# A gated cross-attention and FFN layer on one core: x loaded transposed with a centred Wq, first loads and projections in parts, sums beside weighted sums, and a list-scheduled FFN tail

## The chip, the cores and the metric

The kernel runs on one core of a Trainium2 chip. The metric is the device time of one execution in microseconds. Three executions of the kernel before took 3187.14, 3182.26 and 3186.66 us, median 3186.66. The core has five instruction queues that this kernel uses: TensorE (PE; its weight loads are listed as PEld), VectorE (DVE), ScalarE (ACT), GpSimd (POOL) and SyncE (SP), which issues every DMA. Each works through its instructions in order and waits on semaphores for the others.

## The reference, cut to what matters

x is 32 sequences of 224 tokens with 512 features, the context 32 sequences of 750 keys with 384 features; 16 heads of 32.

```python
q = layernorm(x) @ Wq.T                       # 16 heads of 32
k, v = ctx @ Wkv.T
attn = softmax(where(mask_of_query, q k^T / sqrt(32), -1e9))
x = x + tanh(g_xattn) * (attn @ v)
h = bitlinear(layernorm(x), w1, b1)           # 512 -> 2048
x = x + tanh(g_ffn) * bitlinear(gelu(h), w2, b2)
# bitlinear: rmsnorm, then each token is rounded to 8 bits with the scale
# 127/max|.|, weights to -1, 0, 1 with the mean of |w|, matmul, bias
```

A token's layernorm needs the mean and variance of its 512 features, a token's rounding needs the maximum of its row, and softmax needs the maximum and the sum over 750 keys.

## The kernel before, in words

The work is a sequence of N = 128 steps (b, g): sequence b and a group g of four heads. Three rows of PSUM tiles matter: `ps_s`, one tile of four banks for scores, and `ps_m`, four tiles of one bank for everything else.

A step has two halves that are worked on in neighbouring steps. `maxima` makes the scores with queries on the partitions, a third at a time (tile sm), and DVE reduces each third to maxima (mx). `minus_max` turns these into three bf16 parts (nb), `turn_max` transposes them (pn, nT). `weights` then makes the scores again with keys on the partitions (tile se: first minus the maximum, by a product with ones, then k by q), ACT takes the exponential (p), and POOL adds the p up over the keys (acc, five additions a step). `values` multiplies v by p (the left half of the tile po), `sums` multiplies ones by acc (the right half of the same po), ACT copies both to oT, and `finish` transposes oT (pyt), divides, and POOL adds the result to x in SBUF; after the last group of a sequence x goes to a DRAM tensor x1_d.

Queries come from `q_units`: DVE takes mean and variance (`stats`), POOL the factor 1/sqrt(variance) times mask and 1/sqrt(32) (`scale`, ve), DVE makes xn = (x - mean) * ve (`apply`), `turn` transposes xn on TensorE in two groups of four (pxn) and ACT copies it (xnT), `q_piece` multiplies by Wq (pq) and ACT copies the result (qT). `k_units` makes k of a step in two halves (pk), `v_piece` makes v in pieces (pv_None, or pv for a half piece).

The FFN takes tiles of 128 tokens in NF = 28 pairs, from `ffn_units`. A pair's first part loads x1_d (`load`, xg), takes statistics, centres (xc), finds the row maximum (amax), rounds (`grid` on POOL, which also adds b2 to xg; `round` on ACT) and transposes by DMA (`turn`, xq to xT). Each of its two tiles t then has four products with w1 (units b, tile ph; DVE scales and adds b1 into h), gelu, square with the sum of squares, row maxima (hm), scales (sb0, sb1, sb2, mostly small POOL operations with a Newton iteration in `rsqrt`), rounding (`cgrid` on POOL, `cround` on ACT, tile hq), a DMA transpose (`cturn`, hT) and two products with w2 (units c, tile po from w2q and hT; DVE adds into xg), after which xg is stored.

The order of all instructions is written out by the loop over steps. Each step has six slots k. In an even slot `maxima` of the next step comes first, in an odd one `weights` of this step; then the units that a `put` marks first, then FFN units as far as they fit, then the other units. So between one sm and the next se (and between se and the next sm), which share the one `ps_s` tile, TensorE has the slot's units to do while DVE reduces or ACT exponentiates. `PE_ROOM` (2.7 us in even, 2.2 in odd slots, less what the slot's units are said to take) limits what FFN work `Ffn.fill` puts in; each FFN unit names the unit that it follows and a lag in slots. In steps 0 to 11 the three odd slots hold the quantisation of w1 and w2 (`weight_units`) in place of FFN units. Slots before: 0 turn_max and the first k half; 1 `values`; 2 the second k half; 3 `sums`; 4 `finish`; 5 a piece of v of the next sequence; slots 3 and 4 also hold half pieces of v (g = 0, 1) or `q_piece` (g = 2, 3), and slots 0 and 2 of g = 1 the two `turn`. Ahead of the loop stand the loads, all q pieces of sequence 0, k of two steps and four pieces of v. Behind it, `fill` is called until the FFN is empty, the newest pair first.

SP takes its DMAs in the order in which these units are written out; a DMA whose data is not there yet holds all behind it.

Of the kernel before, what the change touches and what calls it, by code (L numbers as in the profile page):

```python
# [24 lines left out]
def flamingo_gated_layer(  # L25
    ctx: ExitStack,
    tc: tile.TileContext,
    x: bass.AP,
    ctxT: bass.AP,
# [45 lines left out]
    x1_d = dram.tile([NT, D], F32, name="x1_d")  # L75

# [30 lines left out]

    def rsqrt(pool, v, n, p, tag):


        y = pool.tile([P, n], F32, tag=f"{tag}_y", name=f"{tag}_y")[:p]
        a = pool.tile([P, n], F32, tag=f"{tag}_a", name=f"{tag}_a")[:p]
        gp.tensor_scalar(
            y.bitcast(I32), v.bitcast(I32), -0.5, float(0x5F3759DF), ALU.mult, ALU.add
        )
        for _ in range(3):
            gp.tensor_tensor(a, y, y, ALU.mult)
            gp.tensor_tensor(a, a, v, ALU.mult)
            gp.tensor_scalar(a, a, -0.5, 1.5, ALU.mult, ALU.add)
            gp.tensor_tensor(y, y, a, ALU.mult)  # L120
        return y
# [18 lines left out]
    np_ = pool("xn", 1)  # L140
# [3 lines left out]
    smp = pool("small", 2)  # L144
    HB, XG = 2, 2
# [3 lines left out]
    fp = pool("f", 1)  # L149
    ps_s = pool("ps_s", 1, PSUM)  # L150
# [13 lines left out]
    x_of, y_of, q_of, k_of, v_of = {}, {}, {}, {}, {}  # L164
# [4 lines left out]
    def load_y(b):  # L169
        y_of[b] = yp.tile([P, NYC, M], F32, tag="y", name=f"y_{b}")  # L170
        sp.dma_start(y_of[b], ctxT[b].rearrange("(c p) m -> p c m", p=P))
# [4 lines left out]


    def q_units(b):

# [3 lines left out]
        xn = np_.tile([CP, NQ, D], F32, tag="xn", name=f"xn_{b}")  # L183
        xnT = np_.tile([P, NDC, S], F32, tag="xnT", name=f"xnT_{b}")
# [13 lines left out]
        def apply():  # L198
            for t in range(NQ):
                dve.tensor_scalar(  # L200
                    xn[:, t, :], x_of[b][:, t, :], mv[:, t, 0:1], ve[:, t : t + 1],
                    ALU.subtract, ALU.mult,
                )

        def turn(c2):
            pt = ps_m.tile([P, 2, NQ, CP], F32, tag="m", name=f"pxn_{b}_{c2}")
            for i in range(2):
                c = 2 * c2 + i
                for t in range(NQ):
                    pe.transpose(  # L210
                        pt[:, i, t, :], xn[:, t, c * P : (c + 1) * P], ident[:CP, :CP]
                    )
            act.copy(xnT[:, 2 * c2 : 2 * c2 + 2, :], pt.rearrange("p c t n -> p c (t n)"))

        def q_piece(g):
            pq = ps_m.tile([P, 512], F32, tag="m", name=f"pq_{b}_{g}")
            for c in range(NDC):
                pe.matmul(
                    pq[:, :S], wq_sb[:, c, g * P : (g + 1) * P], xnT[:, c, :],
                    start=(c == 0), stop=(c == NDC - 1),  # L220
                )
            act.copy(qT[:, g, :], pq[:, :S])

        return [stats, scale, apply], [lambda i=i: turn(i) for i in range(2)], [
            lambda g=g: q_piece(g) for g in range(NG)
        ]
# [153 lines left out]
    def sums(b, g):  # L380
# [7 lines left out]
        oT = smp.tile([P, 2 * S], F32, tag="oT", name=f"oT_{b}_{g}")  # L388
# [3 lines left out]
    def finish(b, g):  # L392
# [11 lines left out]
        yo = smp.tile([CP, NQ, P], F32, tag="yo", name=f"yo_{b}_{g}")  # L404
# [8 lines left out]
        if g == NG - 1:  # L413
            sp.dma_start(
                x1_d[b * S : (b + 1) * S, :].rearrange("(t p) d -> p t d", p=CP), x_of[b]
            )
# [73 lines left out]
    def quant_scales(s, r, amax, n, tag, unit):  # L490
# [7 lines left out]
        gp.tensor_tensor(a, r, amax, ALU.mult)  # L498
        gp.tensor_scalar(a, a, 1e-5, None, ALU.max)
# [3 lines left out]
        gp.tensor_scalar(c, c, 127.0, None, ALU.mult)  # L503
        gp.tensor_tensor(c, c, r, ALU.mult)
        gp.tensor_scalar(a, a, unit, None, ALU.mult)

    def ffn_units(i):
# [6 lines left out]
        def a_load():  # L514
            s["xg"] = xgp.tile([P, TG, D], F32, tag="xg", name=f"xg_{i}")
            sp.dma_start(s["xg"], x1_d[rows, :].rearrange("(t p) d -> p t d", p=P))
# [8 lines left out]
        def a_rsqrt():  # L525
# [4 lines left out]
            gp.tensor_scalar(s["nm"], s["mv"][:, :, 0], -1.0, None, ALU.mult)  # L530
            gp.tensor_scalar(ve, s["mv"][:, :, 1], 1.0 + EPS, EPS * EPS, ALU.mult, ALU.add)
# [18 lines left out]
        def a_grid():  # L550
            for t in range(TG):
# [3 lines left out]
                )  # L555

# [33 lines left out]
        def b_square(t):  # L590
            h = s["h", t]
            junk = fp.tile([P, F], BF16, tag="xc", name=f"junk_{i}_{t}")
# [9 lines left out]
        def c_scales(t, k):  # L602
            if k == 0:
# [3 lines left out]
                gp.tensor_scalar(u, s["ssq", t], 1.0 / F, EPS, ALU.mult, ALU.add)  # L607
# [12 lines left out]
        def c_turn(t):  # L620
            s["hT", t] = fp.tile([P, NFC, P], BF16, tag="hT", name=f"hT_{i}_{t}")
            sp.dma_start_transpose(s["hT", t], s.pop(("hq", t)))

        def c_matmul(t, half):
# [8 lines left out]
            if half:  # L633
                at = (i * TG + t) * P
                sp.dma_start(out[at : at + P, :], s["xg"][:, t, :])
# [10 lines left out]
            ("grid", 0, "sa2", 0, 0, 0, a_grid),  # L646
            ("round", 2, "grid", 0, 1.1, 0, a_round),
# [3 lines left out]
        for t in range(TG):  # L651
            part = []
            for f in range(4):
                part.append((
                    f"b{t}{f}", 0 if f else 3, f"b{t}0" if f else "turn", 0.9, 0, 0.75,
# [12 lines left out]
            for a in range(2):  # L668
# [3 lines left out]
                ))  # L672
            parts.append(part)
        return parts

    class Ffn:
# [9 lines left out]
        def ready(self, pair, unit):  # L686
            name, lag, after = unit[:3]
            if after is not None:
                at = self.at.get((pair, after))
                if at is None or self.slot < at + lag:  # L690
                    return False

            before = {
                "load": [(pair - XG, f"c{TG - 1}1")],
# [4 lines left out]
            if name[-1].isdigit():  # L699
# [7 lines left out]
                    f"cturn{t}": [(p1, f"c{t1}1")],  # L707
                }
            if name.startswith("square") and any(
# [41 lines left out]
        def done(self):  # L751
            return self.next == NF and not self.parts
# [146 lines left out]
```

## Time and profile before

The profiled execution took 3185.84 us, its span from first to last instruction is 3184.1 us, and the mean granted TensorE clock 0.984.

| Stretch, us | TensorE busy | DVE busy | ACT busy | POOL busy | granted clock |
|---|---|---|---|---|---|
| 0 to 44.7, ahead of the step loop | 31.8 | 13.1 | 6.8 | 4.1 | 1.00 |
| 66 to 150 | 81.0 | 51.1 | 31.5 | 47.3 | 1.00 |
| 150 to 350 | 182.9 | 134.8 | 71.8 | 118.8 | 0.97 |

Groups that the change touches: 256 transposes pxn, 259 ns each; 64 scalings xn, 1153 ns; 64 copies xnT, 532 ns; 128 copies qT, 345 ns; 1024 matmuls po from acc and ones. DMAs, median time to landing: x 448 KB 6.9 us, y 1125 KB 6.3, x_d 448 KB 3.1, xg 512 KB 3.6, out 256 KB 2.0, xT 2.5, hT 4.3.

Busy shares count an engine's instructions, and ends of matmuls are modelled. A wait is put down to the engine whose signal came last. "xN" is a number of instructions, and letters such as pk, sm, se, po are the tiles written. The line L51 is that of a helper (`Ordered`), which records every operation, so lines don't tell operations apart and tile names do.

### The profile page before, as it was taken

The page shows a single profiled execution, that of the slowest core. Times are in us where ns is not written, and L with a number is a line of the kernel's source. Part 1 is how long each engine was busy: PE and PEld are TensorE (multiplying, and loading weights), DVE is VectorE, ACT ScalarE, POOL GpSimd, SP SyncE. Part 2 cuts the span into 40 slices and gives each one's busy share as a digit, 9 for nine tenths or more (in the row PEclk, how much of TensorE's full clock was granted, in tenths as well). Part 3 has the DMA queues.
Part 4 walks back from the last instruction along what each step waited for, and adds up shares of the span by engine and source line. Part 5 has one row for each costly group of instructions (what it writes and reads, how often), then busy time and mean ns, then how long its engine had stood idle before and what let it go on. Part 6 is the DMA issues. An engine that isn't in the chain of part 4 may idle for free.

```text
span 3184.1 us, 63629 instructions
## 1 busy us (share of the span) xinstructions
PE 2996.3 (94%) x27522; PEld 1920.3 (60%) x27522; DVE 1705.7 (54%) x2501; ACT 1515.2 (48%) x1663; POOL 2069.3 (65%) x3048
## 2 busy tenths in 40 slices
PE   7998999999999999999999999999999999999963
PEld 5655556666666666666666666666666666666632
DVE  4676555555555555555555455465555554555442
ACT  2333444554545445544554454455444545554542
POOL 2564667766676676666766666776667667666672
PEclk9999999999999999999999999999999999999976
DMA  3322122011211111122011211111121011111111
GB/s 130 100 79 75 37 50 64 17 51 47 57 51 32 39 45 50 42 55 56 21 48 42 56 41 50 37 41 48 47 57 51 23 47 45 50 46 31 37 36 43
DMA packets 199753, 157.09 MB, mean 49 GB/s; under 512 B 150832, under 2 KB 150832, under 8 KB 199344
## 3 DMA queue, kind: packets, MB, share of 16 engines
q1 hardware_dynamic: 199472, 153.03, 17.4%
q8 instruction: 215, 3.52, 0.5%
q14 instruction: 66, 0.54, 0.1%
HBM read 86.94 MB, written 29.36 MB: 37 GB/s over the span
## 4 chain that ended last, share of the span: by engine, by line
PE 77%; DVE 14%; ACT 4%; POOL 3%; issue 1%; DMA 1%; SPq 0%; ACTq 0%; POOLq 0%; DVEq 0%
PE po L51 16%; PE se L51 13%; PE sm L51 12%; DVE mx L51 11%; PE pk L51 10%; PE pv_None L51 9%; PE ph L51 6%; PE pq L51 4%; PE pv L51 4%; ACT p L51 2%; ACT L51 1%; POOL acc L51 1%; PE pyt L51 1%; DVE xn L51 1%; PE pxn L51 1%
## 5 line engine op out<-in xcount | busy, mean ns | idle before, releaser
L51 POOL TENSOR_TENSOR acc<-acc,p 125x896 f32<-125x896 f32 x512 | 1070.1, 2090 | 462.8 <-ACT p L51 442.3
L51 DVE TENSOR_REDUCE mx<-sm 112x4 f32<-112x2000 f32 (+1 forms) x384 | 860.9, 2242 | 924.5 <-PE sm L51 924.5
L51 ACT ACTIVATE p<-se 125x1792 f32<-125x1792 f32 x384 | 638.9, 1664 | 426.4 <-PE se L51 416.3
L51 PE MATMUL pk<-y,wkv_sb 128*128 128x375 f32 x1536 | 537.7, 486 | 15.2 <-DMA wkv_sb<-in_wkvT 12.2
L51 ACT COPY kT<-pk 128x375 f32<-128x375 f32 x256 | 120.8, 472 | 716.8 <-PE pk L51 716.8
L51 PE MATMUL sm<-kT,qT 32*112 32x500 f32 (+1 forms) x4096 | 426.7, 508 | 30.2 <-ACT p L51 29.6
L51 POOL TENSOR_TENSOR acc<-p 125x896 f32<-125x896 f32 x128 | 267.1, 2087 | 257.4 <-ACT p L51 257.0
L51 PEld LDWEIGHTS pk<-y,wkv_sb 128*128 128x128 f32 x1536 | 278.7, 190 | 177.5 <-issue 32.9
L51 PE MATMUL pv_None<-wkv_sb,y 128*125 128x256 f32 x1536 | 366.1, 389 | 0.0
L51 PE MATMUL se<-qT,kT 32*125 32x224 f32 x6144 | 364.8, 349 | 0.0
L51 PEld LDWEIGHTS pv_None<-wkv_sb,y 128*125 128x125 f32 x1536 | 279.3, 188 | 70.9 <-issue 34.2
L51 PE MATMUL po<-p,v 125*32 125x224 f32 x6144 | 321.3, 358 | 0.1
L51 PEld LDWEIGHTS se<-qT,kT 32*125 32x125 f32 x6144 | 299.4, 183 | 0.2
L51 PE MATMUL po<-w2q,hT 128*128 128x256 fp8e4 x1792 | 224.6, 281 | 60.1 <-DMA hT<-hq 60.1
L51 DVE SCALAR_TENSOR_TENSOR h<-ph,qa_am,b_sb 128x512 f32<-128x512 f32 x224 | 164.8, 743 | 203.3 <-PE ph L51 202.2
L51 PEld LDWEIGHTS sm<-kT,qT 32*112 32x112 f32 x4096 | 159.2, 170 | 166.1 <-issue 99.9
L51 PEld LDWEIGHTS po<-p,v 125*32 125x32 f32 x6144 | 187.8, 111 | 115.6 <-issue 40.1
L51 PEld LDWEIGHTS <-hT 128*128 128x128 bf16 x1792 | 174.2, 101 | 104.2 <-DMA hT<-hq 62.3
L51 PE MATMUL ph<-w1q,xT 128*128 128x512 fp8e4 x896 | 226.8, 382 | 4.8 <-DVE h L51 4.8
L51 PE MATMUL pq<-xnT,wq_sb 128*128 128x224 f32 x1024 | 219.3, 357 | 0.2 <-ACT xnT L51 0.2
L51 PE MATMUL se<-nT,ones 3*125 3x448 bf16 x1536 | 157.4, 396 | 64.6 <-DVE mx L51 60.7
L51 POOL TENSOR_TENSOR x<-x,yo 112x256 f32<-112x256 f32 x128 | 100.9, 788 | 159.0 <-DVE yo L51 112.0
(96 smaller groups left out, 3207.6 us busy)
## 6 DMA issues: line engine op xcount, KB each, us to landing
y<-in_ctxT SPq DMA_DIRECT2D x32, 1125.0 KB, 6.3
x<-in_x SPq DMA_DIRECT2D x32, 448.0 KB, 6.9
x_d<-x SPq DMA_DIRECT2D x32, 448.0 KB, 3.1
xg<-x_d SPq DMA_DIRECT2D x28, 512.0 KB, 3.6
out<-xg SPq DMA_DIRECT2D x56, 256.0 KB, 2.0
wa<-in_w1T SPq DMA_DIRECT2D x8, 512.0 KB, 4.5
wa<-in_w2T SPq DMA_DIRECT2D x8, 512.0 KB, 4.0
wb<-in_w1T SPq DMA_DIRECT2D x8, 512.0 KB, 3.8
```

The lines of the kernel that those rows point to most:

```text
L51: return lambda *args, **kw: tc.keep_in_program_order(build(*args, **kw))
```

## The change

A second copy of x, transposed to features by tokens, is handed to the kernel (xT), and loaded per sequence into one SBUF tile. The mean is taken out of Wq instead of x: `centre` multiplies ones by Wq for its column sums and subtracts 1/512 of them. So `q_piece` multiplies the centred Wq by x^T, and each token's factor is applied to the product by DVE. The factor lies with tokens on partitions and is needed along the free dimension in all partitions; `spread` writes it to DRAM and reads it back to all partitions (for sequence 0 by a product with the identity). `apply` and `turn` are gone.

The first loads come in parts, the first 128 columns of Wkv and Wq and half of y first. Two q pieces of sequence 0 and all v pieces go into the steps' slots (`put_values`; one slot more in steps 0, 2, 3 and 4). The second k half moves from slot 2 to 1, `values` and `sums` stand together in slot 2, the store of x in slot 5. Small operations are fused where they have one column. The FFN's `bias` and `out` become units of their own, squares have their own tile, hT has two. The last pair is loaded from x in SBUF. After the loop `drain` writes all that is left of both pairs in an order chosen by estimated times (`TAKES_US`): among the units that can start within 1 us of the soonest, the one with the longest path behind it. The small operations then run on DVE instead of POOL.

```diff
+        m = pool.tile([P, n], F32, tag=f"{tag}_m", name=f"{tag}_m")[:p]
+        gp = small[0]
         gp.tensor_scalar(
             y.bitcast(I32), v.bitcast(I32), -0.5, float(0x5F3759DF), ALU.mult, ALU.add
         )
+        gp.tensor_scalar(m, v, -0.5, None, ALU.mult)
         for _ in range(3):
+            if n == 1:
+                gp.tensor_scalar(a, y, y, m, ALU.mult, ALU.mult)
+                gp.tensor_scalar(y, a, 1.5, y, ALU.add, ALU.mult)
+                continue
             gp.tensor_tensor(a, y, y, ALU.mult)
-            gp.tensor_tensor(a, a, v, ALU.mult)
-            gp.tensor_scalar(a, a, -0.5, 1.5, ALU.mult, ALU.add)
+            gp.tensor_tensor(a, a, m, ALU.mult)
+            gp.tensor_scalar(a, a, 1.5, None, ALU.add)
             gp.tensor_tensor(y, y, a, ALU.mult)
         return y
...
+    def load_xT(b):
+        xT_of[b] = xtp.tile([P, NDC, S], F32, tag="xT", name=f"xTb_{b}")
+        sp.dma_start(xT_of[b], xT[b].rearrange("(c p) s -> p c s", p=P))
+
+    def centre(lo, hi):
+
+
+        pw = ps_m.tile([P, 512], F32, tag="m", name=f"pwq_{lo}")
+        for c in range(NDC):
+            pe.matmul(
+                pw[:, : hi - lo], ones, wq_sb[:, c, lo:hi], start=(c == 0), stop=(c == NDC - 1)
+            )
+        for c in range(NDC):
+            dve.scalar_tensor_tensor(
+                wq_sb[:, c, lo:hi], pw[:, : hi - lo], -1.0 / D, wq_sb[:, c, lo:hi],
+                ALU.mult, ALU.add,
...
+        def spread():
+            if b == 0:
+                pr = ps_m.tile([P, NQ, CP], F32, tag="m", name="prb")
                 for t in range(NQ):
-                    pe.transpose(
-                        pt[:, i, t, :], xn[:, t, c * P : (c + 1) * P], ident[:CP, :CP]
+                    pe.matmul(
+                        pr[:, t, :], ve[:, t : t + 1].to_broadcast([CP, P]), ident[:CP, :CP],
+                        start=True, stop=True,
                     )
-            act.copy(xnT[:, 2 * c2 : 2 * c2 + 2, :], pt.rearrange("p c t n -> p c (t n)"))
+                act.copy(rb, pr.rearrange("p t n -> p (t n)"))
+                return
+            with nc.allow_non_contiguous_dma(reason="one number of each token"):
+                sp.dma_start(r_d[b].rearrange("(t p) -> p t", p=CP), ve)
+            sp.dma_start(rb, r_d[b].partition_broadcast(P))
...
-                    pq[:, :S], wq_sb[:, c, g * P : (g + 1) * P], xnT[:, c, :],
+                    pq[:, :S], wq_sb[:, c, g * P : (g + 1) * P], xT_of[b][:, c, :],
...
+            dve.tensor_tensor(qT[:, g, :], pq[:, :S], rb, ALU.mult)
...
+            if i < NF - 1:
+                sp.dma_start(s["xg"], x1_d[rows, :].rearrange("(t p) d -> p t d", p=P))
+                return
+            at = rows.start
+            while at < rows.stop:
+                (q, p), (t, to) = divmod(at, CP), divmod(at - rows.start, P)
+                n = min(CP - p, P - to)
+                sp.dma_start(
+                    s["xg"][to : to + n, t, :], x_of[q // NQ][p : p + n, q % NQ, :]
+                )
+                at += n
...
+    def store(b):
+        sp.dma_start(
+            x1_d[b * S : (b + 1) * S, :].rearrange("(t p) d -> p t d", p=CP), x_of[b]
+        )
...
+        def drain(self):
+
+
+            small[0] = dve
+            free = dict.fromkeys(("PE", "ACT", "DVE", "POOL", "SP"), 0.0)
+            end = {}
+
+            def takes(name):
+                kind = name.rstrip("0123456789")
+                return TAKES_US.get(kind + name[-1]) or TAKES_US[kind]
+
+            while self.next < NF:
+                self.parts += [[self.next, part] for part in ffn_units(self.next)]
+                self.next += 1
+            left = {}
+
+            def rank(at):
+
+                if at not in left:
+                    left[at] = 0.0
+                    left[at] = sum(us for _, us in takes(at[1])) + max(
+                        (rank(x) for x in behind if at in behind[x]), default=0.0
+                    )
+                return left[at]
+
+            behind = {
+                (pair, u[0]): [(pair, u[2] or "")] + self.behind(pair, u[0])
+                for pair, units in self.parts for u in units
+            }
+            while self.parts:
+                self.slot += 10
+                found = []
+                for part in self.parts:
+                    for unit in part[1]:
+                        if self.ready(part[0], unit):
+                            at = part[0], unit[0]
+                            since = max(
+                                [end.get(x, 0.0) for x in behind[at]
+                                 if x[1].rstrip("0123456789") not in ORDER_ONLY
+                                 or x[1][:-1] != at[1][:-1]], default=0.0,
+                            )
+                            since = max(since, free[takes(unit[0])[0][0]])
+                            found.append((since, -rank(at), part, unit))
+                soon = min(f[0] for f in found) + 1.0
+                at, _, part, unit = min((f for f in found if f[0] <= soon), key=lambda f: f[1])
+                part[1].remove(unit)
+                self.at[part[0], unit[0]] = self.slot
+                unit[6]()
+                for engine, us in takes(unit[0]):
+                    at = max(at, free[engine])
+                    free[engine] = at + (0.1 if engine == "SP" else us)
+                    at += us
+                end[part[0], unit[0]] = at
+                self.parts = [p for p in self.parts if p[1]]
+            return end
...
     load_x(0)
-    load_y(0)
-    sp.dma_start(wkv_sb[:, :, :D], w_kv[:, :, :D])
-    sp.dma_start(wq_sb, wqT.rearrange("(c p) e -> p c e", p=P))
+    sp.dma_start(wkv_sb[:, :, :P], w_kv[:, :, :P])
+    load_y(0, 2)
+    sp.dma_start(wq_sb[:, :, :P], w_q[:, :, :P])
+    load_xT(0)
+    sp.dma_start(wkv_sb[:, :, P:D], w_kv[:, :, P:D])
...
+    V_MORE = {0: 2, 2: 1, 3: 1, 4: 1}
...
-            put(1, 2.3, lambda: values(*last), first=True)
-            put(3, 0.5, lambda: sums(*last), first=True)
+            put(2, 2.7, lambda: (values(*last), sums(*last)), first=True)
             put(4, 0.5, lambda: finish(*last), first=True)
+            if last[1] == NG - 1 and last[0] < B - 1:
+                put(5, 0.0, lambda: store(last[0]), first=True)
...
-            put(2, 1.9, ks[1])
+            put(1, 1.9, ks[1])
...
+        if n in V_MORE:
+            put_values(V_MORE[n])
+        if n < 2:
+            put(4, 1.5, q0[n + 2])
+        if n < N and g < 2:
+            put_values(3, 4)
+        if n < N:
+            put_values(5)
...
-    while not ffn.done():
-        ffn.fill((1.9, 9.0, 9.0), B, newest=True)
+    ffn.drain()
```

## The prediction

> **What bounds the kernel now.** I read the page's first two parts, then busy time by stretch, then the waits, then the chain for single pieces. The page:
>
> ```profile
> PE 2996.3 (94%) x27522; PEld 1920.3 (60%) x27522; DVE 1705.7 (54%) x2501; ACT 1515.2 (48%) x1663; POOL 2069.3 (65%) x3048
> PE   7998999999999999999999999999999999999963
> PEclk9999999999999999999999999999999999999976
> ```
>
> TensorE is near full in all but the first and the last two of the 40 slices, and only there is there much to win besides its work itself. Busy time by stretch (us and share columns per engine, then clock, DMA share, GB/s), from 350 us to just before the end, and the last 106 us:
>
> ```profile
> 350.00:3000.00 2650.00, 2580.39 (x23920) 1658.26 (x23919) 1427.85 (x2116) 1330.87 (x1456) 1795.85 (x2671) 1.00 0.17 45
> 3000.00:3078.00 78.00, 62.13 (x620) 37.28 (x620) 36.35 (x60) 38.40 (x35) 56.64 (x86) 0.85 0.13 34
> 3078.00:3184.00 106.00, 40.11 (x220) 23.94 (x212) 29.21 (x48) 28.41 (x22) 35.43 (x107) 0.71 0.19 44
> ```
>
> In the middle TensorE idles 70 us of 2650 (2.6%); in the last 106 us it idles 66. Who it waits for over the whole span (total, times, longest):
>
> ```profile
> PE se L51 <- DVE mx L51: 60.7, 153, 4.8
> PE po L51 <- DMA hT<-hq: 60.1, 5, 25.0
> PE sm L51 <- ACT p L51: 29.6, 40, 1.9
> PE pk L51 <- DMA wkv_sb<-in_wkvT: 12.2, 1, 12.2
> PE po L51 <- POOL acc L51: 3.3, 1, 3.3
> ```
>
> So there are three places: 12.2 us before the first matmul, small waits between a score product and its reduction or exponential (se, sm), and 60 us for transposes of the FFN's hidden rows, 58.9 of them after 3078 us. Pieces of the chain show a step's parts and the serial path of a tail tile:
>
> ```profile
> 66.23 1.95 PE pk L51 x6
> 68.19 0.39 PE pxn L51 x4
> 68.57 1.10 PE se L51 x20
> ...
> 3108.43 1.98 POOL h L51
> 3110.44 2.01 ACT hq L51
> 3112.47 4.31 DMA hT<-hq
> 3116.82 5.57 PE po L51 x32
> ```
>
> **The change, part by part.** All sums are on the profiled span of 3184.1 us; its execution took 3185.84, 1.7 more, and the median shown is 0.8 above that.
>
> *x^T from DRAM, Wq centred.* This removes 256 transposes (pxn), 64 scalings (xn), 64 copies (xnT). A step that held a group of four transposes is longer by 0.39 us (row above: pk ends 68.18, se starts 68.57), two groups per batch: 0.78. The group's busy sum, 35.0 us, counts overlap, so I take 0.78. In the 26 batches from step 20 to the last that TensorE bounds: -20 us. I cut the timeline at each start of sm and se into six gaps per step, one for each slot; in steps 20 to 119 those that held a group (slots 0 and 2 at g=1) waited 0.3 us in all, so nothing was hidden there and the 0.78 counts fully. DVE gains 128 products qT<-pq,rb; nearest row yo<-pyt,rd, 112x256 from PSUM, 424 ns: +54 us, against 71.2 us of xn taken away, and ACT loses 44+34 us. None is the bound: 0. What could be late: the x^T tile is single. It is asked for in slot 5 of step g=1 and used in slot 3 of g=2; four slots of 3.94, 4.31, 3.81 and 4.11 us (mean start to start) are 16 us, and x, of equal bytes, lands in 6.9, so SP may be 9 us late.
>
> *Each batch's factor through DRAM.* SP gets a write r_d of 224 numbers and a read rb that waits for it, in front of x_d, hT, out and xT. Neither is in the trace. Nearest row: SP waits for x_d<-x 45.1 us in 16 times, 2.8 us each. [...] By the row SP stands 2.8 us per batch[...]; I bound it by double, 5.6. Both fit in the 9 us above and in the FFN's three slots between transpose and matmul (11.8 us against 4.3 of hT): 0 in the sum by either; without the cover 31 times 2.8 to 5.6, 87 to 174 us.
>
> *Sums beside weighted sums.* values moves from slot 1 to 2, sums from 3 to 2, the second k piece from 2 to 1. The new sums would wait for POOL's last addition acc. I set each step's end of acc against the end of its middle sm plus 2.4 us of values: least margin 1.2 us, median 7.5. No wait. Slot 2 now holds 2.48+0.59 us after its sm, over the 2.35 that reduction and hand-over take, so its 7.9 us of waits (steps 20 to 119) go. Slot 1 falls from 2.45 to 1.95 us and slot 3 loses 0.5, so exponentials delayed by a 1.28 us table load show more: they cost 11.0 and 6.2 us there now. The planned order puts FFN matmuls in 48 of 100 gaps of slot 1 (15 before), 50 in slot 3 (52), 55 in slot 4 (52), 60 in slot 0 (70). I take +5 against -8: -3, between -25 and +15.
>
> *Head.* The loads move 0.37 to 0.40 MB per us from 6 us on (busy time by 2 us stretches). The first k piece needs x, 128 columns of Wkv and half of y, 1.23 MB where it needed 2.40; with the lag that the old load had behind its bytes it starts at 9.2 instead of 12.2. The two k pieces take 6.9 us where later ones take 2.05 each. [...] the row says 2.7, and I keep the row for both kernels. [...] Then 16.1 prb, 16.6 column sums (8 passes, 0.19 us weight loads: 1.5), four DVE subtractions at 0.3 (TensorE waits 1.2), pq 1.75, its product 0.4: the first sm is at 21.4 (22.3 before). Two k pieces, 8 passes for the other 384 columns (0.34 each as pk: 2.7), four subtractions of 0.57 with TensorE waiting 2.3, pq, sm, its reduction: step 0's first sm at 38.2, 44.7 before: -6.5. The four more issues on SP (0.45 us each) hide behind these bytes: the rest of Wq lands near 15 us and is wanted at 27. The scaling of Wv now stands ahead of that sm's reduction: +1.3. Put off into steps 0 to 4: four v pieces (pv_None, 2.8 us each on the chain at 62 and 83 us: 11.2) and two pq (3.5), less 3.5 us of waits that they and the new slots fill and 0.8 of transposes: +10.4. Steps 5 to 19 gain 0.2 of pxn and 0.2 of waits each: -6. Sum: -0.8.
>
> *End of attention.* Fused small operations: a hidden tile's scales go from 19 operations to 12 on POOL, at a pitch of 0.27 us (start to start on the chain) 1.9 us. One such tile stands on the chain between 3044 and 3063 us: -2. Elsewhere POOL is not waited for: 0. The FFN's other edits (own tile for the squares, two hT tiles, bias and store as units, x_d one slot later) move units between slots; TensorE waits for no hT between 350 and 3000 us, and that slack hides them: 0.
>
> *Tail.* In both orders pairs 26 and 27 are left. Now, from the last exponential's end (3077.7) it takes 106.4 us: each pair's tiles run one after another. Next, on the same rows, us after that point: last acc 4.3; x's addition now stands behind pair 26's grid (1.4) and bias (2.5): 10.6; four SBUF copies land at 14.5 (x_d 3.1 and xg 3.6 are gone). Pair 26: round 8.6, two transposes 12.3, ph to 19.5 with DVE holding its second tile for pair 27's mean and scale (16 operations at 0.2), so second tile 24.7. DVE's maxima and scales end at 30.5 and 31.8; grid of 27 33.2, of 26's first tile 35.2; hq 37.2, hT 41.5, po from 42.5 to 47.7 while 27's first ph has run. 27's second ph to 51.2, po of 26's second tile 56.4. 27's scales 59.9, grid 61.9, hq 63.9, hT 68.2, po 73.8; hq is a single tile, so second hq 70.2, hT 74.5, po 80.1, add and store 83.5. So -23, between -10 (no overlap, only fewer hops and smaller scales) and -40 (DVE and ACT run densely). I used cold po rows (5.6 us for 32; warm 1.92 for 16)[...].
>
> Sum: -20 -3 -0.8 -2 -23 = -49; span 3135, time 3137.5 on the median's footing. A difference of 0.2% (6 us) is what a measurement of this kernel can tell.
>
> **The rivals.** *Waits shrink too:* TensorE's 70 us in the middle fall by a third as DVE and ACT lose work, and the tail gives 35: 3137-20-12=3105. For: xn takes 956 ns at the median and 536 at least, so it met something; against: half of the waits stand in slot 4, whose filling hardly changes.
>
> *Little more than the transposes:* tail gives 10 and slots 1 and 3 wait 12 us more: 3137+13+12=3162. For: chain-like dependence of a tile (grid, hq, hT, po are 13.9 us); against: two pairs now alternate.
>
> *Slower:* SP. If r_d and rb, held by POOL's factor and by stores, make x^T land late, TensorE stands in slot 3 of 31 steps. It decides from 49/31=1.6 us per batch, that is SP 10.6 us late on average; at 2.5 us past that: 3137+31*2.5=3215. For: SP is one queue with 99 more DMAs; against: its issues take 0.3 to 0.5 us each at rest.
>
> *The list scheduling doesn't overlap, and x^T saves nothing* because score, reduction, score, exponential bind a step: 3*(1.1+2.25+1.2+1.67)=18.7 us plus hand-overs against 23.8 per step. Excluded in the middle; only with an opening 10 us worse does it come to no change.
>
> **How the numbers follow.** Forecast 0.55 (own range 3122 to 3152), waits shrink 0.18, little more 0.15, no change 0.03, slower 0.09. Faster 0.88, same 0.03, slower 0.09. The range runs to both neighbouring cases: 3104 to 3166.
>
> **What would show it.** Right: first pk near 9.2 us; step 0's first sm near 38; no pxn; no wait of po for acc in the middle; PE waits from 350 to 3000 us between 45 and 85 us; the last exponential some 26 us earlier, and 83 from there to the end, hT waits under 45 us. Wrong: pq waiting for xT or rb, step length unchanged, or a tail over 96 us.

## The result, and the profile after

The changed kernel takes 3148.19 us (median of four executions, 3142.71 to 3151.39), the kernel before in the same comparison 3184.72 us: a ratio of 0.9884, 95% interval 0.9866 to 0.9901. The forecast was 3137 us with a range of 3104 to 3166. The profiled execution of the changed kernel is the fastest of its four, 3142.71 us with a span of 3140.9; against the span before of 3184.1 that is 43.2 us less, where the sum of the prediction had 49. Where stages are compared below, they are stages of the profiled executions.

The page of the changed kernel, busy times and the rows of 40 slices:

```profile
PE 2967.4 (94%) x27286; PEld 1898.8 (60%) x27286; DVE 1712.2 (55%) x2642; ACT 1454.8 (46%) x1471; POOL 2031.1 (65%) x2647
...
PE   7988999999999999999999999999999999999974
...
PEclk9998999999999999999999999999999999999987
```

TensorE lost 29 us of busy time. The third and fourth slices (157 to 314 us) are 8 where the middle is 9 (before, the third was 9): the opening is what the change left worst. The waits of TensorE over the whole span (total, times, longest):

```profile
PE se L52 <- DVE mx L52: 56.5, 123, 3.9
PE sm L52 <- ACT p L52: 51.4, 66, 3.1
PE po L52 <- DMA hT<-hq: 15.6, 4, 11.8
PE ph L52 <- DVE qb_am L52: 15.6, 1, 15.6
PE pk L52 <- DMA y<-in_ctxT: 9.4, 1, 9.4
```

Waits for hT fell from 60.1 to 15.6 us, the first wait from 12.2 to 9.4; waits for exponentials (sm for p) grew from 29.6 to 51.4. Busy time by stretch, with the columns of the table before (PE, PEld, DVE, ACT, POOL, then clock, DMA share, GB/s):

```profile
350.00:3000.00 2650.00, 2576.95 (x23977) 1653.61 (x23974) 1432.52 (x2192) 1292.82 (x1304) 1798.57 (x2390) 1.00 0.21 51
3000.00:3062.00 62.00, 43.95 (x472) 27.97 (x464) 24.43 (x43) 29.82 (x25) 40.54 (x57) 0.78 0.15 39
3062.00:3141.00 79.00, 39.25 (x220) 22.39 (x220) 41.10 (x118) 28.77 (x22) 21.37 (x20) 0.71 0.24 54
```

The tail after the last exponential is 79 us with 39 of TensorE, where it was 106 with 40. In the middle TensorE idles 73 us of 2650, as before (70): the gain there is removed work, not removed waits. The stages, cut at the first sm in slot 0 of a step, against the terms of the prediction:

| Stage, us | before | after | difference | predicted |
|---|---|---|---|---|
| to step 0's first sm | 44.7 | 35.0 | -9.7 | -6.5 |
| steps 0 to 11 | 266.6 | 289.5 | +22.9 | +8.9 |
| steps 12 to 123 | 2671.1 | 2639.4 | -31.7 | -26.2 |
| step 124 to the last exponential's end | 95.3 | 98.1 | +2.8 | -2 |
| tail | 106.4 | 78.9 | -27.5 | -23 |

(The column on the right splits the 6 us that "steps 5 to 19" were to gain by the number of steps into 2.8 and 3.2 us, and has the 1.3 us for Wv in steps 0 to 11.) One term is far off: steps 0 to 11 lost 14 us more than forecast. The cut at step 124 is not clean: of the matmuls with w2, 16 (one product, about 1.9 us) stand behind it that stood ahead of it before, so about 1.9 us of the 31.7 are work that moved into the next row.

### The profile page after: what moved, and what is told of

It is laid out like the page before. It is cut to its first block, busy times and chain, and to the rows that moved or that the text cites. A ratio compares the mean times of both kernels' runs of the same rounds, so it can differ in the third digit from the quotient of the medians.

```text
span 3140.9 us, 63064 instructions
## 1 busy us (share of the span) xinstructions
PE 2967.4 (94%) x27286; PEld 1898.8 (60%) x27286; DVE 1712.2 (55%) x2642; ACT 1454.8 (46%) x1471; POOL 2031.1 (65%) x2647
## 4 chain that ended last, share of the span: by engine, by line
PE 77%; DVE 11%; ACT 8%; POOL 3%; issue 1%; DMA 1%; SPq 0%; ACTq 0%; DVEq 0%; POOLq 0%
PE po L52 17%; PE se L52 13%; PE sm L52 12%; PE pk L52 11%; PE pv_None L52 9%; DVE mx L52 8%; PE ph L52 6%; ACT p L52 6%; PE pv L52 3%; PE pq L52 2%; ACT L52 1%; POOL acc L52 1%; PE pyt L52 1%; DVE wb L52 1%; PE pn L52 0%
## 5 line engine op out<-in xcount | busy, mean ns | idle before, releaser
L52 PE MATMUL pk<-y,wkv_sb 128*128 128x375 f32 x1536 | 546.5, 492 | 9.4 <-DMA y<-in_ctxT 9.4
L52 PE MATMUL sm<-kT,qT 32*112 32x500 f32 (+1 forms) x4096 | 427.0, 508 | 59.0 <-ACT p L52 51.4
L52 PE MATMUL ph<-w1q,xT 128*128 128x512 fp8e4 x896 | 230.2, 387 | 19.4 <-DVE qb_am L52 15.6
L52 PE MATMUL po<-w2q,hT 128*128 128x256 fp8e4 x1792 | 220.0, 278 | 15.6 <-DMA hT<-hq 15.6
L52 ACT COPY oT<-po 128x448 f32<-128x448 f32 x128 | 68.1, 532 | 338.0 <-PE po L52 338.0
L52 PE MATMUL pq<-xTb,wq_sb 128*128 128x224 f32 x1024 | 219.8, 358 | 1.1 <-DVE wq_sb L52 0.7
L52 PE MATMUL se<-nT,ones 3*125 3x448 bf16 x1536 | 157.6, 398 | 56.5 <-DVE mx L52 56.5
```

What stands on the lines that cost most here:

```text
L52: return lambda *args, **kw: tc.keep_in_program_order(build(*args, **kw))
```

## The experiments

All times are medians; the kernel before took 3184.9 to 3186.0 us in these comparisons.

### x^T alone, and the same without the trip through DRAM

Edit of the first, in the kernel before (`load_xT`, `centre` and `q_units` are those of the change; slots, store, FFN and tail stay as before):

```diff
-    for unit in norm + ks[:2] + turns + qs[:1]:
+    for unit in norm[:2] + ks[:2] + norm[2:]:
         unit()
+    centre(0, D)
+    qs[0]()
...
-            put(0, 0.25, turns[0])
-            put(2, 0.25, turns[1])
+            put(5, 0.0, lambda: load_xT(b + 1))
```

> The kernel before with x^T and the centred Wq alone (factor through DRAM, product with it on DVE); order of slots, tail and the rest of the opening are those of before. The head must pay for column sums over all 512 columns at once: by the rows of the changed kernel 1.07+2.74 us of matmuls and 4 subtractions of about 0.7 us, against two groups of transposes and their copies, so about +3 us. Theory A, transposes at 0.78 us a batch as forecast: 30 batches x 0.78 = 23 us less, plus 3: about 3165 (step 12 to step 124: 2671 us before, 22 less). Theory B, the whole 31.8 us that steps 12 to 124 lost in the changed kernel (1.14 us a batch) comes from this part: about 3153 to 3156. Theory C, r_d and rb hold SP and x^T comes late: 3180 or more, with waits of pq for xT or of qT for rb.

Measured: 3266.21 us, ratio 1.0257 (1.0242 to 1.0273): in the range of theory C, but not with the waits that it named. The part that was to bring 20 us makes the kernel 81 us slower when it stands alone. It is the slower case of the rivals, but at another place: no engine shows a wait for x^T or for rb. SP's own instructions in one batch of that run (start, duration, operation):

```profile
652.59 0.33 SPq L52 DMA_DIRECT2D x_d<-x  x1
652.96 0.46 SPq L52 DMA_DIRECT2D r_d<-ve  x1
663.17 0.34 SPq L52 DMA_DIRECT2D rb<-r_d  x1
663.62 3.16 SPq L52 DMA_TRANSPOSE hT<-hq  x1
```

rb cannot be issued before r_d has landed, and SP stands 10.2 us (9.2 on average over 31 batches). The hidden tile's transpose, ready meanwhile, is behind it; between 500 and 3100 us TensorE waits for it:

```profile
PE po L52 <- DMA hT<-hq: 45.8, 7, 8.8
```

The second kernel replaces the trip by the product that sequence 0 has:

```diff
-            if b == 0:
+            if True:
                 pr = ps_m.tile([P, NQ, CP], F32, tag="m", name="prb")
```

> The run with x^T alone took 3266 us: SP stood 262 us behind r_d in 30 batches (8.7 us each, the longest 10.9), and TensorE waited 46 us more for hT in the middle, and 27 us went in steps 4 to 12, where the weight loads stand behind r_d on SP. Here the same kernel hands each sequence's factor to all partitions by the product with the identity that sequence 0 has, and nothing goes through DRAM; TensorE has two more products a batch for it (about 0.43 us by the row of prb, 13 us in all, in steps 4 to 124). Theory A, the hold on SP is the whole loss: 3185 + 3.5 (head) - 23 to 32 (transposes) + 9 to 13 (products) = 3166 to 3178, no hT waits in the middle. Theory B, x^T's own load, or the product on DVE, is what comes late: 3230 or more, with the same waits.

Measured: 3193.76 us, 1.0029 (1.0018 to 1.0040). Neither expectation held. The trip through DRAM cost 72 us and its waits for hT are gone; but 9 us of loss are left. The stages say where: steps 12 to 123 take 2665.3 us, which with 28 groups of prb at a pitch of 0.43 us (12.0 us, the start of prb to that of the next product) makes, as an estimate, 2653.3 for x^T itself: 17.8 us less than before, or 0.64 us a batch (0.78 predicted; it counts all that x^T moves on the other engines too). Against it stand 3 us at the head and 12.3 us in steps 0 to 11 (278.9 against 266.6), though this kernel moved no work there. That is half of what the changed kernel lost in the opening, and neither the trip on SP nor the moved pieces made it.

### What the opening lost: quantisation beside POOL's additions

The timeline of the kernel before at the end of step 6 (DVE and POOL, and the first product se behind the reduction):

```profile
190.28 0.74 DVE L51 TENSOR_SCALAR wb<-wb,wscale 128x1024 f32<-128x1024 f32 x1
...
191.06 1.10 DVE L51 TENSOR_SCALAR wb<-wb 128x1024 f32<-128x1024 f32 x1
191.62 4.96 POOL L51 TENSOR_TENSOR acc<-acc,p 125x896 f32<-125x896 f32 x2
192.20 2.46 DVE L51 TENSOR_SCALAR w1q<-wb 128x1024 fp8e4<-128x1024 f32 x1
...
194.57 2.23 DVE L51 TENSOR_REDUCE mx<-sm 112x4 f32<-112x2000 f32 x1
...
196.86 0.41 PE L51 MATMUL se<-nT,ones 3*125 3x448 bf16 x4 [1.21 <-DVE mx L51]
```

and the changed kernel at the same place:

```profile
194.04 0.38 DVE L52 TENSOR_TENSOR qT<-pq,rb 128x224 f32<-128x224 f32 x1
...
194.34 1.14 DVE L52 TENSOR_SCALAR wb<-wb,wscale 128x1024 f32<-128x1024 f32 x1
195.39 4.56 POOL L52 TENSOR_TENSOR acc<-acc,p 125x896 f32<-125x896 f32 x2 [0.46 <-ACT p L52]
195.51 2.50 DVE L52 TENSOR_SCALAR wb<-wb 128x1024 f32<-128x1024 f32 x1
...
198.05 2.44 DVE L52 TENSOR_SCALAR w1q<-wb 128x1024 fp8e4<-128x1024 f32 x1
...
200.42 2.23 DVE L52 TENSOR_REDUCE mx<-sm 112x4 f32<-112x2000 f32 x1
...
202.70 0.41 PE L52 MATMUL se<-nT,ones 3*125 3x448 bf16 x4 [3.29 <-DVE mx L52]
```

A quantising operation takes 0.69 to 0.75 us alone (medians of 16) and about 2.45 us beside POOL's additions. Before, one of three met them and another met their start; now qT's product (0.38 us, ACT's copy before) is ahead of them on DVE, two of three meet them fully, and the reduction is 2.08 us later: TensorE waits 3.29 us in place of 1.21. It does so in steps 7, 8 and 11, to within 0.4 us, in every run that has x^T and these slots, the two above too. The reduction out of PSUM doesn't stretch: mx is 2.23 to 2.24 us in both. The 2.45 - 0.69 = 1.76 us more are less than one addition (2.09 us here); what makes them, no run here shows.

The test puts the weight units behind the reduction in place of ahead of the next one:

```diff
-                if k in (1, 3, 5):
+                if k in (0, 2, 4):
                     wunits.pop(0)()
```

> The changed kernel with the weight units of steps 0 to 11 (sums of |w|, quantisation) in the three even slots in place of the odd ones, so that on DVE they stand behind the reduction of a score product and not just ahead of the next one. Theory A, steps 7 to 11 are long because quantising operations that run beside POOL's additions take 2.4 to 2.5 us in place of 0.7 to 1.1 and hold the reduction: the waits of slot 0 in steps 4 to 11 (16.4 us, of which about 8 are the step's usual 1 us) fall by 7 to 9 us, and the clock no longer dips: 3138 to 3141. Theory B, the opening is long by its moved work (a fifth piece of v, 2.8 us) and by the clock alone: 3148 within 3 us. Theory C, in even slots the quantisation delays nb or the k copies instead: 3150 or more, with waits in slots 1 to 5.

Measured: 3137.69 us, 0.9851 (0.9837 to 0.9866), 10.5 us below the changed kernel's median and just under the range of theory A. The waits of steps 7, 8 and 11 are 1.50 to 1.51 us (that of step 9 is 4.62 us in place of 3.85; it was 4.85 in the kernel before). Steps 0 to 11 take 282.2 us, where four other profiled kernels with the opening of the changed one took 292.4 to 293.8, at a granted clock between 130 and 340 us of 0.96 against 0.92 to 0.93. (The changed kernel's own profile, its fastest execution, has 289.5 us and 0.95.) So the place of the quantisation is shown as a cause, and theory B fell. A quantising operation of 2.46 us is still there, and no longer in front of a product that waits.

In that run pwm waits 3.8 us for the sum of |w|, made in the same unit (0.8 in the changed kernel). With the sum one unit earlier

```diff
         def between():
             fetch(*every[0], "wb")
-            mean()
-        units.append(between)
+            dve.tensor_reduce(tot, parts, AX.X, ALU.add)
+        units += [between, mean]
```

> The weight units in even slots and the sum for the mean a unit ahead, without the late rule (3128.4 with it). Theory A: the late rule costs 2 us, as alone (3150.2 against 3148.2): 3126. Theory B: with an opening this short the late rule helps: 3130 or more.

3128.49 us were measured, 0.9818 (0.9803 to 0.9833), between the two theories: steps 0 to 11 take 275.4 us at a clock of 0.98. More than the wait came back, 9 us for 3.8. This is 20 us below the changed kernel.

How the lost time splits into waits and clock can be read from the traces. Steps 0 to 11 of six runs (start:end, length, then the columns of the table before): the kernel before; x^T with the product; the changed kernel; a run below whose opening is that of the changed kernel (small operations on POOL); the weight units in even slots; these with the sum ahead.

```profile
44.72:311.28 266.56, 245.11 (x2271) 155.49 (x2270) 176.44 (x227) 94.07 (x116) 146.22 (x115) 0.98 0.26 84
47.73:326.61 278.88, 252.69 (x2259) 158.22 (x2259) 181.78 (x233) 88.28 (x101) 144.04 (x115) 0.95 0.26 85
35.01:324.55 289.54, 261.87 (x2311) 167.96 (x2311) 185.71 (x243) 89.64 (x100) 146.48 (x118) 0.96 0.28 83
35.95:329.69 293.74, 268.01 (x2310) 171.06 (x2311) 185.17 (x243) 89.56 (x100) 145.25 (x118) 0.94 0.27 82
35.88:318.06 282.18, 260.16 (x2311) 167.12 (x2311) 182.75 (x247) 89.64 (x100) 146.97 (x118) 0.96 0.29 85
36.09:311.54 275.45, 256.85 (x2311) 165.38 (x2311) 181.18 (x243) 89.63 (x100) 147.18 (x118) 0.98 0.29 87
```

The traces' records of the granted clock hold two values, 1.00 and 0.50. It stood at 0.50 for 10.2, 27.3, 23.9, 37.5, 20.5 and 13.6 us of these six stretches. The last four hold the same matmuls, and TensorE's busy time for them rises with the time at half clock, from 256.9 to 268.0 us. So the gap between the even slots and the four kernels with the changed opening is 4 to 5 us of waits and 5 to 8 us of busy time at the lower clock; of the 6.7 us that the sum ahead brings in steps 0 to 11, about half is busy time. The 12.3 us that x^T with the product loses are 4.7 us of waits and 7.6 of busy time, for twelve matmuls fewer. In the changed kernel's trace each of the five pieces at half clock begins 2.8 to 5.2 us after the start of a wait of TensorE of 1.80 to 3.85 us, but one wait of 3.29 us has no such piece behind it. The waits come first and the clock adds to them; which wait brings it down isn't shown.

### The store of x, and the second hT tile

Two edits that the prediction costed at nothing could be what keeps the trip of the factor harmless in the changed kernel. There, SP writes

```profile
630.85 0.53 SPq L52 DMA_DIRECT2D r_d<-ve  x1
637.73 0.33 SPq L52 DMA_DIRECT2D rb<-r_d  x1
638.15 0.38 SPq L52 DMA_DIRECT2D x_d<-x  x1
```

that is, the store x_d comes after rb, and the stand is 6.9 us (7.2 on average).

```diff
-    htp = pool("hT", 2)
+    htp = pool("hT", 1)
...
-                    f"cturn{t}": [(ph, f"c{th}1")],
+                    f"cturn{t}": [(p1, f"c{t1}1")],
```

> The changed kernel with one hT tile, and a hidden tile's transpose behind the products of the tile just before it, as in the kernel before. I had costed the second hT tile at nothing. Theory A, it is what keeps SP's stand for r_d (6.6 us a batch) from reaching TensorE, as it reached it with x^T alone: 30 to 50 us of waits for hT in the middle and 6 us more in the tail: 3180 to 3205. Theory B, other edits (the store of x one slot later, bias and out as units) keep it away, and the second tile helps the last tiles alone: about 3154. Theory C, it does nothing: 3148 within 3 us.

3150.02 us, 0.9888 (0.9873 to 0.9902), in theory C's range: no loss that can be told from the changed kernel. The middle (500 to 3000 us) has 1.1 us of hT waits; but the tail is 85.2 us in place of 78.9, the 6 us that theory B had. The store is another matter:

```diff
             if last[1] == NG - 1 and last[0] < B - 1:
-                put(5, 0.0, lambda: store(last[0]), first=True)
+                put(4, 0.0, lambda: store(last[0]), first=True)
```

> The changed kernel with the store of x back in slot 4, ahead of r_d on SP, as it stood with x^T alone. From the issue of r_d to that of rb SP stood 9.2 us on average with x^T alone, where the write x_d is just ahead, and 7.2 us in the changed kernel, where x_d comes after rb; and there x_d also waits for POOL's last addition to x first. Theory A, the slot of the store is what separates the two: r_d to rb takes 9 us again, hT is late in some pairs (25 to 46 us of waits in the middle), and the weight loads of steps 4 to 12 are late: 3175 to 3220. Theory B, the store costs nothing by itself, it took the other orders of before (FFN units, two hT tiles, slots of sums) to make hT late: within 4 us of 3148, even where r_d to rb is 9 us.

3174.18 us, 0.9961 (0.9947 to 0.9976): 26 us, close under the range of theory A, and well outside B. One slot of one store decides 70% of the change's gain. Its mechanism is for the most part not the one I expected first, hT (6 us of waits in the middle), but the weight loads. SP stands 8.5 us on average from r_d to rb. Around 160 us of that run:

```profile
152.63 0.45 SPq L52 DMA_DIRECT2D r_d<-ve  x1
...
160.88 0.34 SPq L52 DMA_DIRECT2D rb<-r_d  x1
...
161.32 3.07 SPq L52 DMA_DIRECT2D wa<-in_w2T  x2
...
166.82 1.22 DVE L52 TENSOR_REDUCE wparts<-wa 128x1 f32<-128x1024 f32 x1 [9.97 <-DMA wa<-in_w2T]
167.96 2.23 DVE L52 TENSOR_REDUCE mx<-sm 112x8 f32<-112x2000 f32 x1
...
170.24 0.64 PE L52 MATMUL se<-nT,ones 3*125 3x448 bf16 x4 [6.25 <-DVE mx L52]
```

The weights are late behind rb, DVE stands 9.97 us for them with the reduction behind, and TensorE 6.25. Between 100 and 345 us DVE stands 18.5 us for weight loads in all, 3.5 in the changed kernel. Steps 0 to 11 take 306.5 us (289.5 in the changed kernel's profile, 292.4 to 293.8 in the four others with its opening), at a granted clock of 0.89 between 130 and 340 us (0.95, and 0.92 to 0.93); steps 12 to 123 take 14.5 us more, 6.4 of them in steps 12 to 19.

Is the second tile a cover only where the store is early? Both edits together:

> The run with the store in slot 4 (3174.2, waits for hT in the middle 6 us) and the run with one hT tile (3150.0, none) joined. With x^T alone, where both stand as before, the middle waited 40 us for hT. Theory A, the two cover the same thing, the trip of the factor ahead of a hidden tile's transpose on SP, and either is enough: joined they lose more than their sum, 3200 to 3220, with 30 us or more of waits for hT between steps 20 and 124. Theory B, the losses add: 3176 to 3178, waits of hT in the middle below 10 us; then the order of the FFN's units, not these two, keeps hT in time.

3177.53 us, 0.9977 (0.9968 to 0.9987): theory B, the losses add. The middle (500 to 3000 us) has 6.6 us of hT waits. So the 46 us that x^T alone has there need something else of the kernel before: the order of the FFN's units, or the slots of k, values and sums. No run isolates which.

### Sums apart from weighted sums

```diff
-            put(2, 2.7, lambda: (values(*last), sums(*last)), first=True)
+            put(1, 2.3, lambda: values(*last), first=True)
+            put(3, 0.5, lambda: sums(*last), first=True)
...
-            put(1, 1.9, ks[1])
+            put(2, 1.9, ks[1])
```

> The changed kernel with values in slot 1, the second k half in slot 2 and sums in slot 3, as before. Theory A, the forecast's: this move is worth little (waits of slot 2 against those of slots 1 and 3): within 3 us of 3148. Theory B, the 10 us by which steps 12 to 124 fell more than 0.78 us of transposes a batch come from this move: 3157 or more. Theory C, the growth of waits in slots 1 and 3 (together 12 us over steps 20 to 119) is larger than what slot 2 gained (8 us): 3144, with slot 2 waiting 8 us again.

3153.13 us, 0.9901 (0.9887 to 0.9916), between theories A and B. Its interval overlaps that of the changed kernel. In steps 12 to 123 it takes 2644.5 us; three kernels with the changed kernel's code up to there took 2639.4 to 2640.6 (with weight units in even slots, and the sum ahead, 2642.4 and 2638.0). But this run does one product with w2 more in these steps (16 matmuls, about 1.9 us), so only 2 to 3 us there can be the move's, hardly more than the kernels differ among themselves. Though waits for p fall to 31.2 us from 51.4, those for mx rise to 66.5 from 56.5: the sum of these waits is 10 us smaller, and the kernel not faster for it.

### The tail

```diff
-    ffn.drain()
+    while ffn.parts or ffn.next < NF:
+        ffn.fill((1.9, 9.0, 9.0), B, newest=True)
```

> The changed kernel with its last units in the order of before: slots filled with lags, newest pair first, small operations on POOL; the last pair still comes from SBUF, bias and out stay units of their own. Theory A, the gain of 27.5 us at the end is mostly the order: about 18 us longer, 3166, tail from the last exponential's end 97 us instead of 79, waits for hT near 55 us again. Theory B, it is the shorter way of x into the last pair and fewer small operations: at most 8 us longer, 3156. Theory C, the order alone gives even more than the whole (the SBUF copies cost): 3176 or more.

3159.52 us, 0.9922 (0.9905 to 0.9938): 11 us, nearer to theory B. The tail is 89.1 us. The waits that come back are few but long:

```profile
PE po L52 <- DMA hT<-hq: 42.8, 5, 23.7
```

So the chosen order is worth 10 us of the tail's 27.5, not most of them. In that run the small operations are on POOL. Leaving them there, with the chosen order (`small[0] = dve` taken out of `drain`):

> The changed kernel with the tail's small operations on POOL (about 0.27 us from start to start) in place of DVE (about 0.2), in the same chosen order. Theory A: 5 chains of 12 to 16 operations stand on the path, each 1 us shorter on DVE, and hops between engines go: on POOL the tail is 4 to 7 us longer, 3153 to 3155. Theory B: on POOL they leave DVE free for the maxima and the additions of h: the tail is shorter, 3144 or less. Theory C: the 10 us that the order of before cost (3159.5) were mostly these operations: 3157 or more.

3145.98 us, 0.9872 (0.9855 to 0.9888): no difference, tail 76.8 us. All three theories named a difference; the engine of the small operations doesn't matter here. The order then is worth 12 us (89.1 against 76.8).

The change also dropped a rule by which the FFN ran closer behind near the end. With it,

```diff
-            return 0.3 * max(0, ready - LATE)
+            return 0.3 * max(0, ready - (LATE if stored < B - 3 else 1))
```

> The changed kernel with the rule of before that lets the FFN run closer behind near the end (LATE of 1 in place of 3 once all but three sequences are stored), which the change dropped. By the written order seven products with w1 of pair 26, a gelu and the rest of its first part then stand ahead of the tail: attention ends 7 x 0.8 = 5.6 us later, and in the tail pair 27's own chain (statistics, norm, maximum, scales, grid) is no longer behind pair 26's work on DVE. Theory A: tail 79 us to 62 to 68, net 5 to 11 us less: 3137 to 3143. Theory B, pair 27's chain binds as it is and the tail falls by no more than attention grows: 3148 within 3 us. Theory C: the products land in slots that are full and the tail stays: 3154.

3150.20 us, 0.9887 (0.9872 to 0.9902): theory B. Steps 100 to the end of attention take 6.4 us more, the tail 4.6 less. And on top of the mended opening

> The changed kernel with the weight units in even slots (that run: 3137.7), with the sum for the mean of |w| one unit ahead of the product that needs it (that run showed TensorE waiting 3.8 us for it), and with the late rule of the run beside it. Theory A, the three are independent: 3137.7 - 3 - (what the late rule alone gives, 0 to 11) = 3124 to 3135. Theory B, the late rule loses what the others gain: 3138 or more.

3128.39 us, 0.9820 (0.9803 to 0.9836), in the range of theory A, and the same as without the rule (3128.49).

## Why the prediction was right or wrong

**Head: right, undersized.** First pk at 9.45 us (predicted 9.2), step 0's first sm at 35.0 (38.2). The two subtraction groups took 0.88 and 1.95 us of DVE; I had 1.2 and 2.3 of waiting, and the two pk 6.05 us in place of 6.9. That last 0.8 us is not the change's: the weight loads of pk follow each other at 0.63 us until the trace's first record of the granted clock, 1.00, at 13.55 us here (4.1 us after the first pk) and at 18.01 before (5.8 us after it), and take 0.19 us in place of 0.34 behind it.

**Steps 0 to 19: wrong, and the only large miss.** The failing step is "steps 5 to 19 gain 0.2 of pxn and 0.2 of waits each: -6", together with "None is the bound: 0" for qT's product on DVE. Steps 0 to 4 lost 13.9 us, where the sum had 11.7. (Four pieces of v were put off into them, as the sum had it; the fifth that an expectation above names isn't in the trace.) Steps 5 to 11 lost 9.1 more in place of gaining 2.8, and steps 12 to 19 gained 0.5 in place of 3.2. The x^T part by itself costs 12 us in the opening: 0.38 us of new DVE work ahead of the quantisation makes 2.08 us of wait in each of three steps, because it moves operations into POOL's additions, and TensorE's clock is at half for 17 us more. A mean of busy time (54% of DVE) doesn't show that. Nor did the forecast ask what waits do to the clock behind the head; in the steps, half clock followed waits of 1.80 and 2.24 us.

**The factor through DRAM: right in the changed kernel, for a reason that was not in the argument.** By the row of x_d I took 2.8 us on SP, and doubled it to 5.6, an estimate of mine with no measured row behind the doubling; it is 7.2 (r_d, 0.9 KB, lands 7.0 us after its issue at the median). The doubling was too small, and no run here tells the size of the pieces from the wait for the landing. TensorE sees none of it, as predicted, and the change of the store's slot, which I costed at nothing ("x_d one slot later"), is what hides it: 26 us. The slower rival named x^T's load as the victim; x^T was never late, and the weight loads and hT were.

**Transposes: right.** -20 predicted from 0.78 us a batch; 0.64 measured, so about -18 for 28 batches.

**Sums beside weighted sums: the guess was of the right size, its working not.** -3 predicted, some 2 to 3 us less measured, hardly clear of the spread. Slot 2's waits went as said (8.0 us in steps 20 to 119); slots 1, 3 and 5 took 13.8 back (slots 0 and 4 lost 4.2), and what was gained is work, not waits: TensorE's idle time in the middle is 73 us (70 before). Of 31.7 us in steps 12 to 123, x^T explains 17.8, the slots 2 to 3 and the moved product 1.9; some 9 us are left, from edits that I had at nothing, and no run isolates them. So the match of -31.7 with -26.2 is in part luck.

**End of attention: wrong.** -2 predicted for one shorter chain of small operations, +2.8 measured. About 1.9 us of that are the product with w2 that moved in from the steps ahead. The late rule that the change dropped isn't it (with it 98.4 us in place of 98.1). The other 3 us of the 4.8 between the two stay open.

**Tail: right, and its parts are not what the heading said.** -23 predicted, -27.5 measured; the first hT of pair 27 lands 65.3 us after the last exponential (68.2 predicted), and the end follows 13.6 us later (15.3). The last pieces of the chain of the changed kernel:

```profile
3118.95 1.98 POOL h L52
...
3120.96 2.01 ACT hq L52
...
3122.98 4.31 DMA hT<-hq
...
3127.34 10.09 PE po L52 x64
```

The first three take what they took before, and po holds the products of two tiles, so the serial path of a tile is as it was; there are fewer of them in a row. List order 10 to 12 us, the second hT tile, costed at nothing, about 6 (the runs overlap and need not add), SBUF copies about 2.6 (from x's end to the first statistics: 9.2 us before, 6.5 after). That leaves some 7 us that no run isolates.

**The rivals.** "Waits shrink too" fell: the middle's idle time is unchanged. "Little more than the transposes" fell with the tail. "No overlap" is half true: the order alone gives 12 us. The slower case is real as a mechanism, and one slot away.

**The marks.** Met: first pk, no pxn, no wait for acc in the middle, 73 us of TensorE idle time between 350 and 3000 us (45 to 85), hT waits of 15.6 us (under 45). Missed: the last exponential ends 15.7 us earlier instead of 26: the opening's 14 us and the 4.8 us at the end of attention, less 3.2 at the head and 5.5 in the steps between; the tail makes up 4.5. So the total, 43.2 us in the profile (36.5 on the medians) for a forecast of 49, is closer than its terms: part of that is luck.

## What to carry to other kernels

A short operation added to an engine at half load was free here only where its place in the order was (0.38 us of product made 2.08 us of wait): look in the timeline at what stands behind it and which other engine that work will then run beside. A DMA whose issue waited for another DMA stopped its whole queue here, for 7.2 us a sequence on average; list everything that is written behind it, and keep large writes from standing just ahead (8.5 and 9.2 us in the two runs with the 448 KB of x there). When a change has many parts, the edits costed at nothing are worth one experiment each: here the slot of one store carried more of the gain than the part that the change is named after.

## What the runs showed of the hardware that was not expected

DVE operations of 128x1024 on SBUF took 0.69 us alone, about 2.45 and up to 3.15 us beside POOL's 125x896 additions, while the reduction out of PSUM beside them kept its 2.24 us. A write of 224 numbers of 4 bytes and the read that waits for it kept SP for 7.2 us on average, and 9.2 us in the run with x^T alone, where a write of 448 KB is just ahead. And the opening lost more to its waits than their length. TensorE's waits in steps 0 to 11, and the granted clock between 130 and 340 us: 34.5 us and 0.89 (store in slot 4), 24.9 to 26.5 and 0.92 to 0.93 (four kernels with the changed opening), 26.8 and 0.95 (the changed kernel's own profile), 21.2 and 0.96, 17.7 and 0.98 (weight units in even slots, without and with the sum ahead). The kernel before has 21.5 us and 0.98, so the sum of the waits alone does not set the clock.
